# Absorbed queries of the third layer by halves of TensorE's rows: four products of 224 columns in place of two of 448

## The chip, the core and the metric

The kernel runs on one core of a Trainium2 chip. The metric is the device time of one execution in microseconds (us); the time of a kernel is the median of several runs. A profiled execution is one further run, recorded by the hardware profiler.

## What is computed

Sixteen sequences of 56 tokens and width 256 pass through four layers, each with cross-attention to a context of 1500 rows of width 128 (`ctx_1024`). The change lies in the third layer (`_L2_xattn_ref`), in its cross-attention with 16 heads of width 8:

```
ckv = encoder_outputs @ ckv_w
ck, cv = jnp.split(ckv, 2, axis=-1)
cq, ck, cv = heads(ci @ cq_w), heads(ck), heads(cv)
cctx = sdpa(cq, ck, cv, causal=False)
hidden_states = hidden_states + merged(cctx) @ cdense_w
```

The kernel does not make the keys. Since `q . (ctx W_k)` is `(q W_k^T) . ctx`, it multiplies each head's query by the head's eight rows of `W_k^T` (it "absorbs" the key weights into the query) and takes the scores against the raw context. All of it is float32.

## The kernel before

Work goes by layer and, within a layer, by groups of `G` = 4 sequences ("batches"). `program` (line 1189) walks 16 items, layer by layer. For each item it runs the attention (`att0`, `att13`, `att2`), and beside it the closing work of the item before and the opening work of the next.

In the third layer, `keys_queries` (line 1023) prepares one batch, 16 times in all:

- It loads the turned context `kt4` (line 113).
- On GpSimd it makes `qs` (lines 1034 to 1038): the batch's 56 queries, 128 rows of 16 heads x 8, repeated for four heads at a time with all rows but the head's own set to zero by the mask `m_heads`. There are four such operations, one for each group `g` of four heads, each with 56 x 4 = 224 columns. In every column only eight of the 128 rows are not zero.
- On TensorE it multiplies two groups at a time (448 columns, 128 rows) by the stationary `ckT`, which is `W_k^T` (line 1041). There are two products for a batch, each into its own buffer `t` in PSUM.
- On ScalarE it copies each result of 448 columns to `qa` (line 1045).

`att2` (line 1090) then runs the scores in periods. One block of `scores_block` (line 339) is four products of 375 columns, one for each quarter of the context, each on 32 columns of the array (the profile writes 128*32). VectorE takes mask and maximum (line 344), ScalarE the exponentials (line 381), VectorE turns the blocks (line 392), and line 1133 forms the weighted sums. `own_sums` (line 1062) closes a batch: its product at line 1071 also goes to a buffer `t`, and VectorE reads that at line 1076. `keys_queries` for the next batch is called in the middle of a batch (line 1115).

Two things set the order around the change. The pool of `t` has two buffers (line 79, `turn` at line 93), which `shift_of` (lines 361 and 373), `values` (line 1055), `own_sums` and `keys_queries` share. And the order on each engine is not the order of the source: the framework's scheduler lays it out when the program is built, by the order of the source, its own durations and the time at which buffers come free in its plan. On the chip each engine then keeps that order, and each instruction waits for its semaphores.

Two more places take part in the argument. `absorbed` (line 692) does the same for the second and fourth layers, with heads of width 64: it already uses the upper or the lower 64 rows of the array (64*128), two halves in two buffers `t`, 112 columns in each product (line 702). And the program holds two variants of itself behind a branch; with these inputs the first one runs (the score tile `ktl` of line 138 is its mark).

Of the kernel before, what the change touches and what calls it, by code (L numbers as in the profile page):

```python
# [9 lines left out]
F32 = mybir.dt.float32  # L10
# [10 lines left out]
B, N, M = 16, 56, 1500  # L21
# [9 lines left out]
NB, BW = 12, 32  # L31
# [8 lines left out]
QC = R // 4  # L40
# [22 lines left out]
def tile_kernel(ctx: ExitStack, tc: tile.TileContext, a, layers=4, groups=NG):  # L63
# [3 lines left out]
    nc = tc.nc  # L67
# [4 lines left out]
    mpool = ctx.enter_context(tc.tile_pool(name="mask", bufs=2))  # L72
# [10 lines left out]
    def psum(pool, tag):  # L83
        return pool.tile([128, 512], F32, tag=tag, name=tag)
# [8 lines left out]
    def turn():  # L93
        return psum(ps_t, "t")
# [16 lines left out]
    def load_kt4(b):  # L111

        kt = kpool.tile([DM, NQ, QB], F32, tag="kt", name="kt4")
        nc.sync.dma_start(kt, a["ctxT4"][b])
        return kt
# [57 lines left out]
    def load_x(gi):  # L173
# [5 lines left out]
    ident = const.tile([128, 128], F32, name="ident")  # L179
    make_identity(nc, ident)  # L180
    sizes = {
        "hm": 26, "m_own": 4, "m_head": BW, "m_eight": 8, "causal": N, "vecs": 22,
        "gates": 4, "rope": 33, "m_mine": H, "m_half": 128, "m_same": BW,
    }
    tables = const.tile([128, sum(sizes.values())], F32, name="tables")
# [4 lines left out]
    hm, vecs, gates = views["hm"], views["vecs"], views["gates"]  # L190
    m_own, m_head, m_eight = views["m_own"], views["m_head"], views["m_eight"]
    causal, tab = views["causal"][:TP], views["rope"][:N]
    m_mine, m_half, m_same = views["m_mine"], views["m_half"], views["m_same"]
    m_self, m_two, m_heads = hm[:, 0:8], hm[:, 8:10], hm[:, 10:26]
    l2w = const.tile([128, 512], F32, name="l2w")
    ckT, cv, cd = l2w[:, :DM], l2w[:, DM : 2 * DM], l2w[:, 2 * DM :]
    no_mask = const.tile([128, QW], BF16, name="no_mask")
# [46 lines left out]
    def scalar_copy(out, in_, scale=1.0):  # L244
        nc.scalar.activation(out, in_, AF.Copy, scale=scale)  # L245
# [777 lines left out]
    def keys_queries(b, state):  # L1023
        made = {}
        state["made"][b % G] = made
        kt = load_kt4(b)
        made["kt"] = kt
        qa = big.tile([128, 2 * R], F32, tag="qa", name="qa2")[:, : 4 * QC].rearrange(
            "p (g n) -> p g n", g=4
        )  # L1030
        made["q"] = qa
        qs = mpool.tile([128, 4, N, 4], F32, tag="mb", name="qs")
        cq = state["cq"][:, b % G * N : (b % G + 1) * N]
        for g in range(4):
            nc.gpsimd.tensor_tensor(
                qs[:, g], cq.unsqueeze(2).to_broadcast([128, N, 4]),
                m_heads[:, 4 * g : 4 * g + 4].unsqueeze(1).to_broadcast([128, N, 4]), ALU.mult,
            )
        for g in range(0, 4, 2):
            p = turn()  # L1040
            nc.tensor.matmul(
                p[:, : 2 * QC], ckT, qs[:, g : g + 2].rearrange("p g n h -> p (g n h)"),
                start=True, stop=True,
            )
            scalar_copy(qa[:, g : g + 2], p[:, : 2 * QC].rearrange("p (g n) -> p g n", g=2))

    def values(made):

# [35 lines left out]
    def first2(gi, state):  # L1084

        cross[gi] = state
        state["made"] = {}
        keys_queries(gi * G, state)

    def att2(gi, state, then, side, ends, last):  # L1090
# [13 lines left out]
        for n in range(per * G):  # L1104
# [4 lines left out]
            if k == 0:  # L1109
                values(made)  # L1110
                den = few_sums()[:, : N // 2].rearrange("p (i g) -> p i g", g=4)
                sums = mpool.tile([128, N, 4], F32, tag="own", bufs=1, name="sums")
            elif k == 2:
                if b + 1 < G:
                    keys_queries(gi * G + b + 1, state)
                else:
                    then()
# [137 lines left out]
def constants():  # L1255

    import numpy as np

    p = np.arange(128)
    head_masks = np.concatenate(  # L1260
        [
            p[:, None] // 16 == np.arange(8), p[:, None] % 32 // 16 == np.arange(2),
            p[:, None] // 8 == np.arange(16),
        ],
        axis=1,
    ).astype(np.float32)

    own = (p[:, None] // 8 % 4 == np.arange(4)).astype(np.float32)  # L1270
    d = np.arange(32)
    head = (p[:, None] % 4 == d // 8).astype(np.float32)
    eight = (p[:, None] % 32 // 4 == np.arange(8)).astype(np.float32)
    t = np.arange(N)
    causal = np.where(t[:, None] >= t[None, :], 0.0, -BIG).astype(np.float32)
    inv = np.float32(1.0) / np.float32(10000.0) ** (np.arange(0, 16, 2, dtype=np.float32) / np.float32(16))
    freqs = np.outer(t.astype(np.float32), inv).astype(np.float32)
    c, s = np.cos(freqs), np.sin(freqs)
    table = np.concatenate([c, c, -s, s, t[:, None]], axis=1).astype(np.float32)

    mine = (p[:, None] % 32 // 2 == np.arange(16)).astype(np.float32)
    half = (p[:, None] % 2 == np.arange(128) // 64).astype(np.float32)
    same = (p[:, None] % 32 == np.arange(32)).astype(np.float32)
    return (
        head_masks, own, head, eight, np.concatenate([causal, causal]), table, mine, half, same
    )


def layout(i):
# [49 lines left out]
    )  # L1341

    masks, own, head, eight, causal, rope, *more = constants()
    vecs = np.concatenate([i[n[:2] + "_xattn" + n[2:]].reshape(2, 128) for n in VEC]).T
    gates = np.concatenate([i[n[:2] + "_xattn" + n[2:] + "_gate"] for n in GATE]).reshape(1, 4)
# [29 lines left out]
```

## Time and profile before

| | us |
|---|---|
| runs: median of 3 (lowest to highest) | 1768.75 (1766.23 to 1775.0) |
| profiled execution, its own time | 1774.53 |
| its span, first to last instruction | 1772.7 |
| around the span | 1.8 |
| PE busy in the span | 1668.2 (94%) |
| DVE busy | 1126.1 (64%) |
| ACT busy | 1022.1 (58%) |
| POOL busy | 112.1 (6%) |
| third layer, about 500 to 1340 us: PE busy | 810.6 of 840.0 |

How to read it: PE is TensorE's products, PEld its loads of stationary operands (they overlap products), DVE is VectorE, ACT is ScalarE, POOL is GpSimd. A float32 product appears as two records, each with its own load. A group's row gives, after the count, the busy time, the mean of one in ns, and the idle time before it with what ended it. The duration of a PE record runs from its start to its modelled end and so contains the array's depth; what a product costs the engine is the step from one start to the next.

### The profile page before, as it was taken

Reading aid. Unit: us, or ns where it says so; the run is one execution under the profiler, and the core shown is the slowest. Engines: PE = TensorE matmul, PEld = TensorE weight load, DVE = VectorE, ACT = ScalarE, POOL = GpSimd, SP = SyncE. Lnnn points to the kernel's source line nnn. Section 1 sums busy time; section 2 is a strip of 40 time slices with the busy share of each in tenths; the row PEclk is TensorE's granted clock in tenths of the full one; section 3 lists DMA queues with packets and bytes.
Section 4 is the critical chain, followed back from the end, with each engine's and each line's share of the span. In section 5 each row is a group of like instructions: output and inputs, shape, how many; then the busy total and the mean of one; then the engine's idle time right before and its main releaser. Section 6 shows DMA issues by size and latency. Waiting matters only on the chain.

```text
span 1772.7 us, 55493 instructions
## 1 busy us (share of the span) xinstructions
PE 1668.2 (94%) x23964; PEld 1104.3 (62%) x23964; DVE 1126.1 (64%) x2742; ACT 1022.1 (58%) x3580; POOL 112.1 (6%) x238
## 2 busy tenths in 40 slices
PE   4888999999999999999999999999999999999997
PEld 2566777776664556545665556556656777777765
DVE  2344866657765666777657776576488746666672
ACT  1443976757454446553755547457555876766663
POOL 0000000000011000110000000000000000000000
PEclk9999999999999999999999999999999999999998
DMA  6431203020030121000210002211200132212120
GB/s 175 126 109 45 77 24 108 25 89 25 14 133 28 43 97 46 21 20 20 99 69 20 20 20 99 74 38 43 99 21 16 48 119 64 76 52 89 44 68 8
DMA packets 60132, 106.80 MB, mean 60 GB/s; under 512 B 7430, under 2 KB 44950, under 8 KB 59878
## 3 DMA queue, kind: packets, MB, share of 16 engines
q1 hardware_dynamic: 58726, 97.01, 17.0%
q0 software_dynamic: 1152, 6.14, 1.4%
q8 instruction: 190, 3.11, 0.7%
q14 instruction: 64, 0.52, 0.1%
HBM read 102.23 MB, written 0.92 MB: 58 GB/s over the span
## 4 chain that ended last, share of the span: by engine, by line
PE 77%; DVE 12%; ACT 6%; DMA 3%; issue 2%; POOL 1%; SPq 0%; POOLq 0%; DVEq 0%
PE sc L339 21%; PE o L795 9%; PE mm L1166 4%; ACT p L381 4%; PE o L1133 4%; DVE p L392 4%; PE mm L858 3%; PE mm L846 3%; PE mm L831 3%; PE mm L682 3%; PE mm L1179 2%; PE t L702 2%; DVE p L344 2%; PE t L1055 2%; PE t L743 2%; PE t L751 2%
## 5 line engine op out<-in xcount | busy, mean ns | idle before, releaser
L381 ACT ACTIVATE p<-p,few 128x96 f32<-128x96 f32 (+1 forms) x1344 | 588.3, 440 | 3.8
L339 PE MATMUL sc<-kt,qa 128*32 128x375 f32 x3584 | 407.8, 486 | 5.1 <-issue 3.1
L392 DVE STREAM_TRANSPOSE p<-p 128x480 f32<-128x480 f32 (+3 forms) x319 | 316.5, 1003 | 53.0 <-ACT p L381 52.1
L344 DVE CUSTOM_DVE_ANT_0 p<-sc,no_mask 128x375 f32<-128x375 f32 x448 | 236.4, 536 | 95.1 <-PE sc L339 86.3
L381 ACT ACTIVATION_READ_ACCUMULATOR p<-p,few 128x1 f32 x1344 | 252.2, 188 | 0.0
L339 PE MATMUL sc<-ktl,qa 128*32 128x96 f32 x7168 | 200.1, 249 | 2.3 <-issue 1.6
L339 PEld LDWEIGHTS sc<-kt,qa 128*32 128x32 f32 x3584 | 126.8, 109 | 107.7 <-issue 70.1
L1133 PEld LDWEIGHTS o<-p,vc 128*32 128x32 f32 x6144 | 142.9, 110 | 75.8 <-issue 51.2
L339 PEld LDWEIGHTS sc<-ktl,qa 128*32 128x32 f32 x7168 | 157.7, 110 | 34.0 <-issue 17.3
L795 PE MATMUL o<-p,kvl 128*128 128x448 f32 x384 | 167.9, 565 | 1.2 <-DVE p L392 1.2
L1133 PE MATMUL o<-p,vc 128*32 128x64 f32 (+1 forms) x6144 | 159.7, 215 | 8.7 <-DVE p L392 7.1
L245 ACT ACTIVATE few<-t 128x14 f32<-128x14 f32 (+2 forms) x128 | 22.2, 174 | 212.7 <-PE t L373 212.7
L350 DVE TENSOR_TENSOR p<-sc,mkl 128x480 f32<-128x480 f32 (+1 forms) x192 | 113.6, 607 | 25.5 <-PE sc L339 25.3
L354 DVE TENSOR_REDUCE few<-p 128x5 f32<-128x480 f32 (+1 forms) x192 | 114.4, 612 | 2.8
L795 PEld LDWEIGHTS o<-p,kvl 128*128 128x128 f32 x384 | 67.0, 191 | 55.3 <-issue 44.7
L245 ACT ACTIVATE qa<-t 128x224 f32<-128x224 f32 (+1 forms) x96 | 38.4, 420 | 91.4 <-PE t L702 62.7
L1166 PE MATMUL mm<-xT,w 128*128 128x224 f32 (+1 forms) x384 | 81.0, 360 | 1.1 <-DVE h2T L1171 0.9
L1166 PEld LDWEIGHTS mm<-xT,w 128*128 128x128 f32 (+1 forms) x384 | 65.7, 178 | 15.6 <-DVE h2T L1171 5.3
L1055 PE MATMUL t<-l2w,kt 128*32 128x128 f32 x1536 | 60.2, 275 | 6.2 <-issue 5.8
L245 ACT ACTIVATE ot<-o 128x448 f32<-128x448 f32 x64 | 33.8, 527 | 54.0 <-PE o L795 54.0
L702 PE MATMUL t<-qT,wl 64*128 64x112 f32 x512 | 55.4, 284 | 3.2 <-DVE qa L713 2.0
L757 DVE TENSOR_TENSOR oT<-t,over 128x224 f32<-128x224 f32 x64 | 31.8, 551 | 41.3 <-PE t L751 38.2
(262 smaller groups left out, 2293.8 us busy)
## 6 DMA issues: line engine op xcount, KB each, us to landing
w<-in_L_W SPq DMA_DIRECT2D x16, 1024.0 KB
kt<-in_ctxT SPq DMA_DIRECT2D x16, 768.0 KB
w<-in_L_Wq SPq DMA_DIRECT2D x8, 1024.0 KB
w<-in_L_Wo SPq DMA_DIRECT2D x8, 1024.0 KB
ktl<-in_ctxT SPq DMA_DIRECT2D x32, 192.0 KB
kvl<-in_ctx_last SPq DMA_DIRECT2D x32, 192.0 KB
w<-in_L_v_qkv SPq DMA_DIRECT2D x4, 768.0 KB
w<-in_L_l_qkv SPq DMA_DIRECT2D x4, 768.0 KB
```

What stands on the lines that cost most here:

```text
L245: nc.scalar.activation(out, in_, AF.Copy, scale=scale)
L339: nc.tensor.matmul(sc[g * BW : (g + 1) * BW, at : at + w], q, k, start=True, stop=True, skip_group_check=True,)
L344: return nc.vector.tensor_tensor_reduce(u["p"][:, i, :w], sc[:, :w], u["mask"], 1.0, LOWEST, ALU.add, ALU.max, u["mx"][:, i : i + 1],).ins ...
L350: nc.vector.tensor_tensor(p, sc[:, : m * w].rearrange("p (i k) -> p i k", i=m), u["mask"].unsqueeze(1).to_broadcast([128, m, w]), ALU.add,)
L354: return nc.vector.tensor_reduce(u["mx"][:, i : i + m], p, AX.X, ALU.max).ins.name
L381: nc.scalar.activation(u["p"][:, i, : u["w"]], u["p"][:, i, : u["w"]], AF.Exp, bias=u["shift"][:, i : i + 1], accum_out=u["den"][:, i : i ...
L392: turned = nc.vector.transpose(blocks, blocks)
L702: nc.tensor.matmul(halves[e][:, j * TP : (j + 1) * TP], wkT[e * 64 : (e + 1) * 64, j0 + j, :], qT[e * 64 : (e + 1) * 64, j0 + j, tok], sta ...
L795: nc.tensor.matmul(o[:, : ub * BW], kv[:, j, :], p, start=start, stop=stop)
L1055: nc.tensor.matmul(p[g * BW : (g + 1) * BW, (j - j0) * DM : (j - j0 + 1) * DM], made["kt"][:, g, j * BW : (j + 1) * BW], cv, start=True, s ...
L1133: nc.tensor.matmul(o[cols, : pieces * BW], made["v"][:, j, cols], p.rearrange("p (i g) r -> p g i r", g=4)[:, g], start=start, stop=stop, ...
L1166: nc.tensor.matmul(p[:w, k * T : (k + 1) * T], wt[:, c, cols], xe[n][:, c, :], start=(c == 0), stop=(c == 1),)
```

## The change

- The mask `m_heads` has 8 columns in place of 16: row `p` counts as head `p // 8 % 8`. The table in memory is narrower by 8 columns.
- `qs` has two groups in place of four. One GpSimd operation now serves two groups of heads at once, since heads `h` and `h + 8` lie in different halves of the rows: two operations for a batch in place of four, of the same 224 columns.
- In place of two products of 448 columns over 128 rows there are four of 224 columns over 64 rows each (`ckT[rows]`, `qs[rows, g]`). Both buffers `t` are taken first. In the source the products alternate: lower half and upper half for `g` = 0, then the same for `g` = 1.
- ScalarE copies as before, two results of 448 columns, now one for each half.

```
-        qs = mpool.tile([128, 4, N, 4], F32, tag="mb", name="qs")
+        qs = mpool.tile([128, 2, N, 4], F32, tag="mb", name="qs")
         cq = state["cq"][:, b % G * N : (b % G + 1) * N]
-        for g in range(4):
+        for g in range(2):
             nc.gpsimd.tensor_tensor(
                 qs[:, g], cq.unsqueeze(2).to_broadcast([128, N, 4]),
                 m_heads[:, 4 * g : 4 * g + 4].unsqueeze(1).to_broadcast([128, N, 4]), ALU.mult,
             )
-        for g in range(0, 4, 2):
-            p = turn()
-            nc.tensor.matmul(
-                p[:, : 2 * QC], ckT, qs[:, g : g + 2].rearrange("p g n h -> p (g n h)"),
-                start=True, stop=True,
-            )
-            scalar_copy(qa[:, g : g + 2], p[:, : 2 * QC].rearrange("p (g n) -> p g n", g=2))
+        halves = [turn(), turn()]
+        for g in range(2):
+            for e in range(2):
+                rows = slice(e * 64, (e + 1) * 64)
+                nc.tensor.matmul(
+                    halves[e][:, g * QC : (g + 1) * QC], ckT[rows],
+                    qs[rows, g].rearrange("p n h -> p (n h)"), start=True, stop=True,
+                )
+        for e in range(2):
+            scalar_copy(
+                qa[:, 2 * e : 2 * e + 2],
+                halves[e][:, : 2 * QC].rearrange("p (g n) -> p g n", g=2),
+            )
...
-            p[:, None] // 8 == np.arange(16),
+            p[:, None] // 8 % 8 == np.arange(8),
```

The built program's order on TensorE, in the variant that runs, is this for a typical batch (buffer, source, output form; line numbers moved by up to 7: 1041 became 1044, 1133 became 1140):

```
before:  L1041 t_7472<-qs 128x448
         L339 sc<-kt4,qa2 32x375 x5
         L1041 t_7475<-qs 128x448
after:   L1044 t_7470<-qs 128x224 x2
         L339 sc<-kt4,qa2 32x375 x5
         L1044 t_7471<-qs 128x224 x2
```

Each buffer name stands for one half. Of the 16 batches, 14 have this form (both products of one half, other work, both products of the other half), one has both products of one half and then, at once, both of the other, and one (the second batch) has the halves alternating.

More of the change, by code (lines that the diff above doesn't have):

```diff
@@ L181, in tile_kernel @@
     sizes = {
-        "hm": 26, "m_own": 4, "m_head": BW, "m_eight": 8, "causal": N, "vecs": 22,
+        "hm": 18, "m_own": 4, "m_head": BW, "m_eight": 8, "causal": N, "vecs": 22,
         "gates": 4, "rope": 33, "m_mine": H, "m_half": 128, "m_same": BW,
@@ L193, in tile_kernel @@
     m_mine, m_half, m_same = views["m_mine"], views["m_half"], views["m_same"]
-    m_self, m_two, m_heads = hm[:, 0:8], hm[:, 8:10], hm[:, 10:26]
+    m_self, m_two, m_heads = hm[:, 0:8], hm[:, 8:10], hm[:, 10:18]
     l2w = const.tile([128, 512], F32, name="l2w")
```

## The prediction

> **What bounds the kernel now.** I read the page first: busy times, slices, and the chain of work that ended last.
>
> ```profile
> span 1772.7 us, 55493 instructions
> ...
> PE   4888999999999999999999999999999999999997
> PEld 2566777776664556545665556556656777777765
> DVE  2344866657765666777657776576488746666672
> ACT  1443976757454446553755547457555876766663
> POOL 0000000000011000110000000000000000000000
> PEclk9999999999999999999999999999999999999998
> ...
> PE 77%; DVE 12%; ACT 6%; DMA 3%; issue 2%; POOL 1%; SPq 0%; POOLq 0%; DVEq 0%
> ```
>
> TensorE is busy in 90% or more of nearly every slice, at its full clock, and holds 77% of the chain. The third layer fills slices 12 to 30. There a saved microsecond of TensorE is worth up to a microsecond, while GpSimd has a tenth of its time in use and 1% of the chain. Second, the groups by line, for the operations that the change touches:
>
> ```profile
> L702 PE MATMUL t<-qT,wl 64*128 64x112 f32 x512 | 55.4, 284 | 3.2 <-DVE qa L713 2.0 <-DVE oT L757 0.9 <-ACT few L245 0.3
> L1035 POOL TENSOR_TENSOR qs<-l,tables 128x224 f32<-128x224 f32 x64 | 37.4, 615 | 78.1 <-PE t L1041 35.7 <-ACT l L245 33.4 <-DVE p L350 9.0
> L1041 PE MATMUL t<-qs,l2w 128*128 128x448 f32 x64 | 31.6, 581 | 0.7
> L1041 PEld LDWEIGHTS t<-qs,l2w 128*128 128x128 f32 x64 | 9.9, 188 | 10.7 <-ACT qa L245 6.7 <-issue 1.2 <-DVE over L1076 1.1
> ```
>
> The 32 products of line 1041 are 64 records; nothing makes TensorE idle long before them (0.7 us), so all that they take is on the path. It is 1.8% of the span: the prize is half of it. Third, the timeline of TensorE, where the start of a row less that of the row before is what the earlier one costs. First one batch of the third layer:
>
> ```profile
> 704.39 1.02 PE L1041 MATMUL t<-qs,l2w 128*128 128x448 f32 x2
> 705.34 1.45 PE L339 MATMUL sc<-kt,qa 128*32 128x375 f32 x10
> 706.88 1.02 PE L1041 MATMUL t<-qs,l2w 128*128 128x448 f32 x2
> 707.83 0.84 PE L339 MATMUL sc<-kt,qa 128*32 128x375 f32 x8
> ```
>
> A product costs 0.95 us. The single records' starts divide this: 0.480 to its second record and 0.469 to the scores, where two records between untiled neighbours step by 0.376. So 0.75 us is streaming and about 0.10 each is paid on entering from, and leaving to, the array in columns. Then two places of line 702, which already works in halves of the rows:
>
> ```profile
> 228.85 1.14 PE L702 MATMUL t<-qT,wl 64*128 64x112 f32 x8
> 229.92 0.29 PE L339 MATMUL sc<-ktl,qa 128*32 128x96 f32 x4
> ...
> 270.74 1.15 PE L702 MATMUL t<-qT,wl 64*128 64x112 f32 x16
> 271.81 0.37 PE L339 MATMUL sc<-ktl,qa 128*32 128x96 f32 x8
> ```
>
> This is the row that decides. Eight records of one half alone take 1.07 us; sixteen, eight of each half, take 1.07 us too. Halves share the time only when both are in the queue together; one half alone leaves the other idle.
>
> **The change, part by part.** *TensorE's order.* In the source the halves alternate. In the built order they do so in one batch of 16. A batch starts with `own_sums` (line 1071) holding one of the two buffers `t` until VectorE has read it, so the scheduler finds a buffer for the lower half, issues both its products, then scores, and the upper half only when ScalarE has copied the lower. In 14 batches other work stands between the halves, in one (the third) the second half waits for VectorE. So the half alone is the case that counts.
>
> *Cost of a half alone.* It is four records of 224 columns. Records of 224 columns step by 0.189 us (lines 682, 846 and 1166 in their runs). A lone half of line 702 pays 0.088 on entering and 0.090 on leaving: 8 x 0.112 + 0.178 = 1.07, as above. So 4 x 0.189 + 0.178 = 0.934 us, against 0.949.
> - 22 products stand between column-tiled work on both sides: 22 x (0.934 - 0.949) = -0.33 us.
> - Four (at 540.5, 546.0, 784.5 and 1002.0 us) follow untiled work and cost 0.845 now. The half must be entered also from there: line 702 after line 954 starts 0.523 later where the untiled step is 0.429. That is 0.094 + 0.934 - 0.845 = +0.18 each, +0.73 us.
> - Two (1141.5 and 1216.5 us) leave to untiled work at 0.856: +0.08 each, +0.16 us.
> - The second batch (579.8 us), halves alternating: two products cost 1.55 us now. Together: 0.094 to enter, two steps of 0.189, 0.178: 0.65 us. Gain 0.90 us, or 0.6 if the upper half starts 0.3 late, as some of line 702's do. I take -0.90.
> - The third batch (644.8 us) takes 1.69 us now, a wait of 0.08 included; two halves one after the other give the same, up to 0.19 less if the last record of the first overlaps. I take 0.
>
> Sum on TensorE: -0.34 us.
>
> *Weight loads.* They double, 64 more records of about 188 ns. One rule speaks against this change. The row first: lone halves of line 702 step by 0.112 us although each load lasts 0.187; eight loads alone would be 1.5 us and the eight records took 1.07. So loads lie under products of the same half. The Trainium skill ("TensorE: Matmul & The Clock Gate", section "The mechanism", on what overlaps) says that a load overlaps running products only when it targets another group of rows. By that rule and the page's load time (columns divided by 1.2 GHz: 0.107 us for 128), a record of 224 columns would step by about 0.296 and the product of 448 by 0.480; a batch half would cost 4 x 0.296 against 2 x 0.480, +0.22 us, and all 32 together +7 us. The row shows 0.376 for the product of 448, and its streaming alone is that (0.189 for half the columns), so no load is in the open. I take the row: 0 us.
>
> *GpSimd.* 32 operations of 0.59 us fall away (19 us of its time). They wait for TensorE or ScalarE, not the reverse: before line 1041 TensorE waited for ScalarE and VectorE, 8 us in all, never for `qs`. In the first batch the lower half needs both new operations, as the first product needed two of the four. Worth 0; without the cover (the half batch of work that lies between) a batch would gain at most two operations, 1.1 us. The shorter table load is 4 KB of 107 MB: 0.
>
> *ScalarE and buffers.* The two copies of 448 columns (543 ns) stay and stand at the same places; the lower half's copy holds back the upper half as the first copy held back the second product (9 waits, 6.7 us in all). Nothing new queues behind them. 0.
>
> *Moved steps.* Elsewhere the order is the same but for single instructions, except from 645 to 690 us. There all four turns of line 252 now stand together and wait for VectorE, the weighted sums and line 846 are interleaved differently, the 0.77 us of scores between line 846 and line 858 comes after line 858 (which waits for Gelu), and ScalarE loads one more table (1.28 us). TensorE is busy in 68.0 of the 70 us from 640 to 710, so a gain is at most 2.0 us, and a loss is bounded by the cover taken away (0.8) plus the table (1.3). I take +0.8, nearest to the row of 0.77.
>
> Total: -0.34 + 0.8 = +0.5 us. On the profiled execution, 1774.5 us by its own time (span 1772.7 and 1.8 around it), that is 1775.0. The median of the runs, 1768.75, is lower by 5.8 us, so I apply the difference to it: **1769.2 us**, no change that could be seen. About 0.5% (8.8 us) is what a measurement of this kernel can tell.
>
> **Rivals.**
> *The halves run together as the source has them* (faster). For: line 702 does it at 270.74 us with no loss. Then a pair costs 2 x 0.189 + 0.178 = 0.56 against 0.95, 0.39 us x 32 = 12.5 us: **1756.3 us**. Against: it needs both buffers free at once; the built order has it in one batch. It would take the engine passing scores that stand ahead in the queue.
> *The loads come into the open* (slower). Place: each half's second, third and fourth record, on the same 64 rows. Price: 64 additional loads x 188 ns = 12.0 us: **1780.8 us**. It decides from 8.8 / 64 = 0.14 us for each additional load, that is, when records in a half step by 0.33 instead of 0.19. By the page's smaller price it is 1775.7 and still within the bound. Against: the 0.112 of line 702.
> *GpSimd's lighter load counts* (slightly faster): 1.1 us in each of the batches where TensorE waits for `qs`; that could be the first alone, so 1768 us, not told from no change.
>
> **How the numbers follow.** The likeliest, halves one after the other at today's price: 0.82, about 1764 to 1777 (the moved steps' bounds -2.0 and +2.1, and the runs of before, which alone spread over 1766.2 to 1775.0). Halves together: 0.07. Loads in the open beyond the bound, or a worse stall in the moved steps: 0.11. The range is widened a little toward both other cases, 1761 to 1778. Faster 0.07, same 0.82, slower 0.11.
>
> **What would show it.** In the changed profile, line 1044 should have 128 records of 224 columns with form 64*128, steps of 0.189 in a half, and busy about the old 31.6 us (30 to 33); rows of it with four records, each starting 0.93 us before the next line's row, and in one place (near 580 us) eight records in 0.65 us. Busy near 18 us would mean halves together; steps of 0.3 or more, loads in the open. GpSimd's row should halve to about 19 us with no change of TensorE's waits. The prediction is wrong if TensorE's busy time or idle time in 640 to 710 us moves by more than 2 us, or if a wait for line 1036 appears before line 1044.

## The result and the profile after

| | before | after |
|---|---|---|
| median of 20 runs each, us | 1769.55 | 1776.19 |
| lowest to highest, us | 1763.48 to 1775.0 | 1767.85 to 1794.85 |
| ratio, 95% interval | | 1.0041 (1.0027 to 1.0055) |
| profiled execution, us (span) | 1774.53 (1772.7) | 1772.88 (1771.1) |
| mean granted clock (before: 47 runs beside the first four experiments; after: without its slowest run) | 0.9879 | 0.9866 |

The change costs 0.4%, about 7 us. One of the changed kernel's 20 executions (1794.85 us, clock 0.978) was in a slower state and is left out of the ratio. The cost is within the 0.5% that the forecast allowed for "no change that could be seen", but the interval leaves out 1, and the sum of the prediction had +0.5 us. The two profiled executions stand the other way round, 1.6 us in favour of the changed kernel. They are one execution each, so the 7 us cannot be read off by laying one against the other.

First the page of the changed kernel: span, TensorE's slices and granted clock, and the engines' shares of the chain.

```profile
span 1771.1 us, 55589 instructions
...
PE   3888999999899999999999999999999899999997
...
PEclk9999999999999999999999999999999999999999
...
PE 76%; DVE 12%; ACT 6%; DMA 2%; issue 2%; POOL 1%; SPq 0%; POOLq 0%; DVEq 0%; ACTq 0%
```

Nothing new bounds the kernel: TensorE is as full as it was, and no other engine has gained a share of the chain. There are 96 more instructions, which is what 64 more records of products, 64 more loads and 32 fewer operations of GpSimd make. Next the groups by line of the changed kernel, for what the diff replaced.

```profile
L1044 PE MATMUL t<-qs,l2w 64*128 64x224 f32 x128 | 31.5, 375 | 0.9 <-ACT qa L245 0.3
L1044 PEld LDWEIGHTS t<-qs,l2w 64*128 64x128 f32 x128 | 20.7, 186 | 11.5 <-ACT qa L245 7.2 <-issue 1.3 <-DVE over L1083 0.8
L1036 POOL TENSOR_TENSOR qs<-l,tables 128x224 f32<-128x224 f32 x32 | 20.1, 648 | 81.3 <-PE t L1044 37.7 <-ACT l L245 33.5 <-DVE p L350 10.0
```

There are 128 records of 64 rows and 224 columns, busy for 31.5 us where 64 records were busy for 31.6. The loads have doubled in number and in time, and the idle time before the products is 0.9 us where it was 0.7. GpSimd has half its operations, and line 1036 is not among what TensorE waited for. Third, the timeline of TensorE in the changed kernel: the second batch, the third batch and a typical one.

```profile
577.06 1.88 PE L954 MATMUL mm<-w,xT 128*112 128x512 f32 x4
578.87 1.03 PE L1044 MATMUL t<-qs,l2w 64*128 64x224 f32 x8
579.83 0.82 PE L339 MATMUL sc<-kt,qa 128*32 128x375 f32 x2
...
642.27 1.86 PE L1044 MATMUL t<-qs,l2w 64*128 64x224 f32 x8
644.06 0.60 PE L252 MATMUL mm<-ident,xn 112*128 112x112 f32 x4
...
738.26 1.02 PE L1044 MATMUL t<-qs,l2w 64*128 64x224 f32 x4
739.21 1.45 PE L339 MATMUL sc<-kt,qa 128*32 128x375 f32 x10
740.75 1.02 PE L1044 MATMUL t<-qs,l2w 64*128 64x224 f32 x4
```

In the typical batch (738.26) a half takes 739.21 - 738.26 = 0.95 us, as long as a product of 448 columns over all rows took; the other half follows 2.5 us after the first. In the second batch, where the halves alternate, eight records take 0.96 us: both halves at the price of one. In the third batch they stand one after the other, 1.79 us.

### The profile page after: what moved, and what is told of

Same layout as the page of the kernel before. It is cut to its first block, busy times and chain, and to the rows that moved or that the text cites. A ratio compares the mean times of both kernels' runs of the same rounds, so it can differ in the third digit from the quotient of the medians.

```text
span 1771.1 us, 55589 instructions
## 1 busy us (share of the span) xinstructions
PE 1666.0 (94%) x24028; PEld 1111.1 (63%) x24028; DVE 1124.8 (64%) x2742; ACT 1023.9 (58%) x3581; POOL 95.1 (5%) x206
## 4 chain that ended last, share of the span: by engine, by line
PE 76%; DVE 12%; ACT 6%; DMA 2%; issue 2%; POOL 1%; SPq 0%; POOLq 0%; DVEq 0%; ACTq 0%
PE sc L339 21%; PE o L795 8%; ACT p L381 4%; PE mm L1173 4%; PE o L1140 4%; DVE p L392 4%; PE mm L858 3%; PE mm L846 3%; PE mm L831 3%; PE mm L682 3%; PE mm L1186 2%; PE t L702 2%; DVE p L344 2%; PE t L1062 2%; PE t L743 2%
## 5 line engine op out<-in xcount | busy, mean ns | idle before, releaser
L350 DVE TENSOR_TENSOR p<-sc,mkl 128x480 f32<-128x480 f32 (+1 forms) x192 | 113.7, 607 | 26.1 <-PE sc L339 25.8
L1062 PEld LDWEIGHTS t<-l2w,kt 128*32 128x32 f32 x1536 | 45.8, 111 | 21.8 <-issue 17.8
```

The costliest lines, as they stand in the source:

```text
L350: nc.vector.tensor_tensor(p, sc[:, : m * w].rearrange("p (i k) -> p i k", i=m), u["mask"].unsqueeze(1).to_broadcast([128, m, w]), ALU.add,)
L1062: nc.tensor.matmul(p[g * BW : (g + 1) * BW, (j - j0) * DM : (j - j0 + 1) * DM], made["kt"][:, g, j * BW : (j + 1) * BW], cv, start=True, s ...
```

## Experiments: where 7 us come from

The prediction's own sum left more than 6 us unexplained. The first theory was that the moved steps between 645 and 690 us cost it all. Its rivals were the products themselves, the mere number of instructions on TensorE, and GpSimd's new operations.

The ratios below are to before, from runs on the same chip; they need not be the quotient of the medians. All were on one chip but `e12`, which with its runs of before was on another. Before itself had 1768.44 us beside the first four kernels, 1767.50 beside the next four, 1768.00 beside `e9`, `e10` and `e11`, and 1767.72 beside `e12`.

**One product of 448 columns for each half** (`e1_half448`). TensorE has before's instructions in before's order; only the rows of these products differ.

```
-        halves = [turn(), turn()]
-        for g in range(2):
...
         for e in range(2):
+            rows = slice(e * 64, (e + 1) * 64)
+            p = turn()
+            nc.tensor.matmul(
+                p[:, : 2 * QC], ckT[rows], qs[rows].rearrange("p g n h -> p (g n h)"),
+                start=True, stop=True,
+            )
```

> The halves of the rows and the two GpSimd operations are kept, but each half is one product of 448 columns, so no product is added and TensorE's order is that of the kernel before, instruction for instruction. Three theories of the +0.4%. Moved steps (the order from 645 to 690 us): gone here, ratio to the kernel before 1.000. More instructions (64 more records with their loads, more code to fetch and more stalls without a visible wait): gone too, 1.000. The half array itself costs more than its steps show: stays, 1.004. By the steps of the changed kernel a half of 448 columns should cost 2 x 0.376 + 0.18 = 0.93 to 0.95 us, as the product before.

Measured: 1769.89 us, ratio 1.0006 (0.9989 to 1.0024). The group by line of this kernel:

```profile
L1043 PE MATMUL t<-qs,l2w 64*128 64x448 f32 x64 | 31.3, 588 | 0.8
```

It shows that half the rows save nothing while the other half has nothing to do: 64 records, 31.3 us, against 31.6 us for all rows. The slowdown is gone as well. So neither the halves as such nor GpSimd's two operations (this kernel has them too) make the 7 us.

**Each product of before cut into two of 224 columns, over all rows** (`e2_split224`). There are no halves here, and TensorE's order is that of the changed kernel, moved steps included.

```
         for g in range(0, 4, 2):
             p = turn()
-            nc.tensor.matmul(
-                p[:, : 2 * QC], ckT, qs[:, g : g + 2].rearrange("p g n h -> p (g n h)"),
+            for k in range(2):
+                nc.tensor.matmul(
+                    p[:, k * QC : (k + 1) * QC], ckT,
+                    qs[:, g + k].rearrange("p n h -> p (n h)"), start=True, stop=True,
...
```

> The kernel before, with each product of 448 columns over all 128 rows made as two of 224; four GpSimd operations stay. It has the changed kernel's number of products and its order on TensorE, moved steps included, but no halves. Moved steps and more instructions: both give the changed kernel's ratio, 1.004. The half array: gone, 1.000 to 1.001.

Measured: 1775.01 us, ratio 1.0038 (1.0022 to 1.0054), the changed kernel's slowdown without any half. What costs is the longer stream of instructions or its order.

**The changed kernel with before's order from 645 to 690 us** (`e3_but_third`). One batch uses a single product of 448 columns for each half, and this is enough for the scheduler to lay out that stretch as before.

```
+        w = 2 if b == 2 else 1
-        for g in range(2):
+        for g in range(0, 2, w):
...
-                    halves[e][:, g * QC : (g + 1) * QC], ckT[rows],
+                    halves[e][:, g * QC : (g + w) * QC], ckT[rows],
...
```

> The changed kernel, but in the third batch of each group each half is one product of 448 columns; this gives back the order of the kernel before from 645 to 690 us, while most of the additional products stay (48 of 64 records). Moved steps: ratio 1.000 to 1.001, and 644.8 to 704.4 us takes 59.6 us as before instead of 61.0. More instructions: 1.003. The half array: 1.004.

The edit reaches only the third batch of the first group, so 60 of the 64 additional records stay, not 48 as the text above says. Measured: 1777.96 us, ratio 1.0061 (1.0037 to 1.0085), above what any of the three theories gave, though the interval reaches down to 1.004. The stretch did come back. These are the starts of the third batch's products and of the next batch's, in before, in the changed kernel and here:

```profile
644.83 1.85 PE L1041 MATMUL t<-qs,l2w 128*128 128x448 f32 x4
704.39 1.02 PE L1041 MATMUL t<-qs,l2w 128*128 128x448 f32 x2
```

```profile
642.27 1.86 PE L1044 MATMUL t<-qs,l2w 64*128 64x224 f32 x8
703.23 1.02 PE L1044 MATMUL t<-qs,l2w 64*128 64x224 f32 x4
```

```profile
640.07 1.85 PE L1045 MATMUL t<-qs,l2w 64*128 64x448 f32 x4
699.80 1.02 PE L1045 MATMUL t<-qs,l2w 64*128 64x224 f32 x4
```

From the one to the other, at full clock in all three, it is 59.56 us in before, 60.96 in the changed kernel and 59.73 here. So the moved steps are worth 1.4 us, and the slowdown stays without them. The first theory falls.

**Four GpSimd operations in the changed kernel** (`e4_pool4`), with TensorE's order untouched.

```
-        qs = mpool.tile([128, 2, N, 4], F32, tag="mb", name="qs")
+        qs = mpool.tile([128, 4, N, 4], F32, tag="mb", name="qs")
...
-        for g in range(2):
+        for g in range(4):
...
-                m_heads[:, 4 * g : 4 * g + 4].unsqueeze(1).to_broadcast([128, N, 4]), ALU.mult,
+                m_heads[:, 4 * (g % 2) : 4 * (g % 2) + 4].unsqueeze(1).to_broadcast([128, N, 4]), ALU.mult,
...
```

> The changed kernel with four GpSimd operations for a batch instead of two (the two additional ones write columns of qs that nothing reads); TensorE's order is that of the changed kernel. All theories: the changed kernel's ratio, 1.004, since GpSimd's lighter load was worth nothing. If GpSimd mattered, it would be slower still, by up to 1 us for each batch (1.01).

Measured: 1778.47 us, ratio 1.0055 (1.0037 to 1.0074). GpSimd has its old load back and the slowdown is still there: GpSimd is not it.

**A new theory: where the packets of code fall.** TensorE stands still at a few places, with "issue" as the reason, that is, with nothing it waits for. This is such a place in before, and then one in the changed kernel, each on TensorE's timeline; the bracket is the idle time before the row.

```profile
937.11 1.27 PE L1055 MATMUL t<-l2w,kt 128*32 128x128 f32 x38
940.95 0.41 PE L1055 MATMUL t<-l2w,kt 128*32 128x128 f32 x3 [2.57 <-issue]
```

```profile
934.48 0.50 PE L1062 MATMUL t<-l2w,kt 128*32 128x128 f32 x7
938.22 2.14 PE L1062 MATMUL t<-l2w,kt 128*32 128x128 f32 x34 [3.24 <-issue]
```

The work stops in the middle of a run of equal products, after 38 of them in one kernel and after 7 in the other. Equal products just before and after it ran without a wait, and the profile shows none here; the theory is that instructions are missing. The stretches of the changed kernel around it (length, busy time by engine, granted clock, the DMA engines' busy share, GB/s) show what else goes on:

```profile
933.00:936.00 3.00, 1.78 (x83) 1.33 (x72) 2.48 (x9) 2.08 (x8) 0.16 (x1) 1.00 0.72 259
936.00:938.00 2.00, 0.00 (x0) 0.00 (x0) 1.39 (x1) 2.00 (x7) 0.00 (x0) 0.96 0.00 0
938.00:941.00 3.00, 2.78 (x44) 2.58 (x47) 0.38 (x1) 1.92 (x7) 0.00 (x0) 0.50 0.02 5
```

From 933 to 936 the DMA engines bring in the next turned context, 768 KB in about 3 us. Code comes by DMA too. The page of the changed kernel has its instructions by engine and this queue (packets, MB, share of the 16 engines):

```profile
PE 1666.0 (94%) x24028; PEld 1111.1 (63%) x24028; DVE 1124.8 (64%) x2742; ACT 1023.9 (58%) x3581; POOL 95.1 (5%) x206
...
q8 instruction: 191, 3.13, 0.7%
```

That is 191 packets of 16 KB, and they are TensorE's: a straight line through them, in before and in the changed kernel, gives one packet for every 256 of its instructions (products, loads and waits). About half of them start 5 to 10 us after the one before. The packet due here is recorded at 935.98, as the load ends, 11.6 us after the one before it, and takes 0.96 us. TensorE goes on at 938.2; the next packet follows after only 3.4 us. All standstills on "issue" of over 0.7 us in the third layer of the two profiles go this way (us from the start of the span):

| kernel | load | code packet starts | TensorE stands |
|---|---|---|---|
| before | 719.5 to 722.5 | 722.3 | 721.9 to 724.6 |
| before | 757.0 to 760.0 | 760.1 | 761.0 to 762.6 |
| before | 935.5 to 938.5 | 938.5 | 938.4 to 940.9 |
| before | 1154.0 to 1157.0 | 1157.2 | 1158.1 to 1159.5 |
| after | 753.5 to 756.5 | 756.5 | 756.4 to 758.8 |
| after | 933.0 to 936.0 | 936.0 | 935.0 to 938.2 |
| after | 973.0 to 976.0 | 976.0 | 976.5 to 978.4 |
| after | 1189.0 to 1192.0 | 1191.7 | 1192.2 to 1193.9 |

Not every packet in such a place stops TensorE. In before 14 packets of the third layer start during one of these loads or within 1 us behind it, in the changed kernel 12, and only four of each go with a standstill. What sets these apart is how late they are. Count TensorE's instructions up to the start of a packet, take off 256 for each packet before it, and call the median of the third layer zero: the eight packets of the table come 241 to 254 instructions late, a whole packet's worth, the other 18 at most 203. So it looks as if TensorE stands where it has used up the code that it had.

A standstill can have an echo: the last row of the stretches has the clock at 0.50. The theory: each 16 KB of code ends at a fixed count of instructions, so any added instruction moves the edges of all later packets against the loads; and a packet that falls due at the wrong place in a load comes so late that TensorE stops. The 64 records and 64 loads that the change adds are half a packet. The rival: more instructions cost time by themselves, wherever the edges fall. Two kernels tell them apart by adding still more instructions.

**32 products of one number each at the start** (`e5_before_s32` on before, `e6_after_s32` on the changed kernel). They are 64 records and 64 loads, half a packet of code, and run while the first loads come in; the rest of the order stays.

```
+        room = mm()
+        for _ in range(32):
+            nc.tensor.matmul(room[:1, :1], ident[:, :1], ident[:, :1], start=True, stop=True)
         load_first()
```

> The kernel before with 32 products of one number each put ahead of everything on TensorE, while it waits for its first data; the order of all else on TensorE is unchanged. Program code reaches TensorE in packets of 16 KB, and these products move the place of every later packet's edge in the program by half a packet or so. Phase of the code packets (stalls come where a packet falls behind a context load; which ones do so depends on the edges): the stalls of the third layer move to other batches, and the time moves by up to 0.4% in either direction (1762 to 1776). Number of instructions in the third layer, or the half array: 1.000, stalls where they were.

> The changed kernel with the same 32 products ahead. Phase of the code packets: the stalls leave the places of the changed kernel, the time moves by up to 0.4% in either direction, most likely down, since the changed kernel has drawn an unlucky phase (1.000 to 1.004 of the kernel before). Number of instructions: stays at 1.004 to 1.006.

Measured: before with them 1773.19 us, ratio 1.0019 (1.0003 to 1.0035); the changed kernel with them 1767.40 us, ratio 0.9994 (0.9978 to 1.0009). The same harmless addition slows the one by 0.2% and takes the whole 0.4% from the other. A cost by number of instructions cannot do that; a shift of packet edges can. In the profile of the changed kernel with the addition, all standstills named in the table are gone, and two of 0.97 and 0.73 us are left. In before with it they moved too, to these two places:

```profile
972.44 0.75 PE L1055 MATMUL t<-l2w,kt 128*32 128x128 f32 x20 [1.43 <-issue]
...
1189.87 0.59 PE L1055 MATMUL t<-l2w,kt 128*32 128x128 f32 x9 [2.20 <-issue]
```

They add up to 3.6 us, where before's four have 8.3, and yet the runs are slower. So standstills are not the whole account. The mean clock of these runs is 0.9854, that of before beside them 0.9884; what that is worth stands further down.

**Both halves side by side** (`e7_stand448`, `e8_ownmm448`). These test the prediction's rival: one product of 448 columns for each half, tied in the scheduler so that the second follows the first at once. In the first kernel the pair waits until `own_sums` has given its buffer back; in the second `own_sums` takes its buffer from the pool `mm` instead.

```
+        before_it = line["over"]
...
-                    halves[e][:, g * QC : (g + 1) * QC], ckT[rows],
-                    qs[rows, g].rearrange("p n h -> p (n h)"), start=True, stop=True,
+                    halves[e][:, : 2 * QC], ckT[rows],
+                    qs[rows].rearrange("p g n h -> p (g n h)"), start=True, stop=True,
...
+                    tc.add_manual_dep(product.ins, before_it,
...
+                before_it = product.ins.name
```

```
+        before_it = None
...
-        t = turn()
+        t = mm()
```

> Halves as one product of 448 columns each, and tied in the schedule so that they are laid out only once VectorE has read the buffer of own_sums: in 12 batches the two halves stand next to each other. If halves share the array's time as those of line 702 do, an adjacent pair takes about 0.95 us in place of 1.90, so 12 x 0.95 = 11 us less, minus 0 to 4 us for the wait for the second buffer and for scores that are moved: ratio 0.994 to 0.998. If halves do not share time: 1.000 to 1.003.

> Halves as one product of 448 columns each; own_sums takes its buffer from the pool of mm, so that both buffers t are free when the halves are due; in nearly all batches they stand next to each other. If halves share time: 14 to 16 x 0.95 = 13 to 15 us less, against what the busier pool of mm costs the side work (0 to 10 us): ratio 0.992 to 1.000. If halves do not share: 1.000 to 1.006.

Measured: the first 1761.61 us, ratio 0.9959 (0.9945 to 0.9972); the second 1785.29 us, ratio 1.0085 (1.0066 to 1.0104). On TensorE's timeline of the first, a pair that finds both buffers free, and one that doesn't:

```profile
742.44 2.14 PE L1045 MATMUL t<-qs,l2w 64*128 64x448 f32 x4
744.51 0.54 PE L1150 MATMUL o<-p,vc 128*32 128x64 f32 x24
...
849.38 1.02 PE L1045 MATMUL t<-qs,l2w 64*128 64x448 f32 x4
850.33 0.48 PE L1150 MATMUL o<-p,vc 128*32 128x64 f32 x19
```

At 849.38 two halves take 0.95 us together; their single records start at 0, 6, 480 and 486 ns, in step. At 742.44 the same four take 2.07 us, since the second had to wait for its buffer. The gain that the halves hold depends on order alone. The kernel has little of it yet: in five of the 16 batches the second half starts within 0.11 us of the first, in six it is next in line but starts 0.5 to 1.2 us after it, and in five other work stands between. Up to the next row the products take 26.1 us, where before's took 29.2, so 3.1 of the 5.9 us between the medians are the halves'. The tie moved other work as well, and where the rest comes from no run separates.

The second kernel is slower than both its expectations allowed. Here the halves share their time in ten batches and their products take 21.6 us, but TensorE is without work for 123 us of its span (1783.5 less 1660.2 busy), against 108 in the first of the two and 105 in before. That the side work which the pool `mm` serves runs later is the likely reason; no row here shows it.

**The standstills taken away.** In `e9_noload` fifteen of the sixteen loads of the turned context are left out; in `e10_pieces` each goes as four transfers of 192 KB. The first leaves all batches with the first one's context. TensorE's order is the changed kernel's in both.

```
+    once = const.tile([DM, NQ, QB], F32, name="once")
...
-        kt = load_kt4(b)
+        if "kt4" not in line:
+            line["kt4"] = once
+            nc.sync.dma_start(once, a["ctxT4"][b])
+        kt = once
```

```
-        nc.sync.dma_start(kt, a["ctxT4"][b])
+        for g in range(NQ):
+            nc.sync.dma_start(kt[:, g], a["ctxT4"][b][:, g])
```

> The changed kernel, but the third layer reads one batch's turned context for all 16 batches: 15 of its 16 loads of 768 KB are left out (so the keys and values of those batches are another batch's). TensorE's order is unchanged. Code packets that fall behind these loads: no stall of TensorE over 0.7 us without a visible wait is left between 600 and 1340 us, and the time falls by the 7 to 9 us that such stalls took, and by half-clock windows that followed them: ratio to the kernel before 0.994 to 0.998. Stalls from code alone, with no part in them of the loads: the stalls stay, 1.003 to 1.006.

> The changed kernel with each load of 768 KB issued as four of 192 KB (one for each quarter of the context, packets of 1.5 KB in place of 6 KB); TensorE's order is unchanged. If a code packet can slip in between the pieces, stalls shrink to under 1 us each: 0.998 to 1.001 of the kernel before. If it waits for all that is queued, stalls stay or grow with the longer load: 1.004 to 1.008.

Measured: without the loads 1767.10 us, ratio 0.9992 (0.9978 to 1.0007); in pieces 1765.91 us, ratio 0.9986 (0.9972 to 1.0000). Both take away the 0.4%. The first was expected to gain more, 0.994 to 0.998. TensorE's timeline at the place of the 3.24 us, in the kernel without loads and then in the one with pieces:

```profile
934.19 1.27 PE L1066 MATMUL t<-l2w,once 128*32 128x128 f32 x39
935.20 0.48 PE L340 MATMUL sc<-once,qa 128*32 128x375 f32 x1
```

```profile
935.06 1.27 PE L1063 MATMUL t<-l2w,kt 128*32 128x128 f32 x39
936.07 0.48 PE L340 MATMUL sc<-kt,qa 128*32 128x375 f32 x1
```

The run that was cut after 7 products goes through 39 without a gap. The first kernel has no standstill of over 0.7 us left in the third layer, the second has one (1.22 us, at 1150.3).

**Pieces alone, on before, and on the pairs** (`e12_before_pieces`, `e11_stand448_pieces`), with the edit just shown.

> The kernel before with its context loads of the third layer in four pieces; TensorE's order is unchanged. It takes the code stalls out of the kernel before too, so that against the changed kernel with the same loads (0.9986 of the kernel before, 1765.9 us) only the change itself is left. By the rows that is +1.4 us for the moved steps and +0.6 us for products and entries: this kernel should take about 1764 us, 0.9975 of the kernel before. If the change costs nothing by itself: 0.9986.

> Halves next to each other as in the tied version, and the load in four pieces. If pieces let code through: 0.992 to 0.995 of the kernel before; if not: 0.996 to 1.000.

Measured: before with pieces 1765.81 us, ratio 0.9995 (0.9983 to 1.0007), which misses its expectation. Two standstills of 1.3 us are left in its profile (715.8 and 1285.0), where before had four of 1.5 to 2.7. The runs gain little by it, at a mean clock of 0.9875 where before's beside them had 0.9892; why the clock was lower is not known. The pairs with pieces take 1759.21 us, ratio 0.9955 (0.9937 to 0.9974), the fastest kernel here, by 0.45% over before and a little short of what was expected; what the pieces add to the pairs is within the intervals. The two kernels with pieces are the fair comparison of the change: 0.9986 against 0.9995 leaves it at -0.09%, give or take 0.18%, so the +2.0 us that the measured terms below give (0.11%) lie just outside, and no loss of 0.4% is left.

## Why the prediction was right or wrong

- **Halves one after the other, no gain: right.** Line 1044's steps in a half alone are 293, 189, 190 and 279 ns, 0.951 us in all. The term was 0.934; entering costs 0.104 where line 702 gave 0.088. Over 22 halves that is 22 x (0.951 - 0.949) = +0.04 in place of -0.33 us.
- **The second batch: a mis-sized term.** It was put at 0.65 us, "two steps of 0.189". A half has four records, not two, since each float32 product is two: with four steps the same sum is 0.094 + 4 x 0.189 + 0.178 = 1.03, and 0.094 + 0.957 = 1.05 was measured. The gain there was 1.55 - 1.05 = 0.50 us, not 0.90, and below the 0.6 that the prediction named as the lower end. The rival "halves together" errs less: its 0.56 us is the price of four records, charged 32 times with entering and leaving each time. Eight records in a row pay that once: both halves take 0.95 us for a batch, against 1.90 for two products, so the rival was worth 0.95 x 16 = 15 us and not 12.5; the pairs of `e7_stand448` that find their buffers free show the price.
- **Entries and exits from untiled work** cost 0.094 us each, as put. All products together: the rows of line 1044 take 29.37 us up to the next row, those of line 1041 took 29.22, and five entries come on top (the second batch's included), 5 x 0.094. That is +0.6 us where the sum had -0.34; 0.1 of it is the third batch, 1.79 against 1.69 us, which was put at 0.
- **Weight loads: right.** The steps of 0.189 us stand beside loads of 0.186 us for the same 64 rows. The rule of the Trainium skill ("TensorE: Matmul & The Clock Gate", section "The mechanism"), that a load overlaps only products on other rows, would have made them about 0.296 by the prediction's estimate. The same section also lets a load into the background weight buffer go ahead, and the steps fit that sentence. The row decided rightly, and the slower rival falls with it.
- **GpSimd, ScalarE and buffers: right.** GpSimd's row fell from 37.4 to 20.1 us without effect, and with four operations instead of two the ratio was 1.0055, within the intervals the same as 1.0041.
- **Moved steps: +1.4 us, not +0.8**, within their bounds (-2.0 to +2.1).
- **What failed is the step from the sum to the total.** It took the rest of the kernel to run as it ran in the profile of before, and put the whole difference into the operations named in the diff. So the standstills for code and the clock, which no term holds, were put at nothing. By measured terms the change is 0.6 + 1.4 = +2.0 us (the third batch's 0.1 stands in both). The medians differ by 6.6. The remaining 4.6 us vanish, and within the intervals the 2.0 with them, when other instructions move the packet edges (`e6_after_s32`), when the loads are left out, and when they are cut. So much is shown: the loss depends on where the code's edges fall and on loads of 768 KB, and the 32 additional products, with their loads half a packet of code, moved those edges. That the range held the time was luck: its width came from the bounds of the moved steps and the spread of before's runs, and nothing in it stood for this cause.

A part of these 4.6 us came by way of the clock. A line through the other 19 runs of the changed kernel (without the one of 1794.85 us) gives about 2 us for each 0.001 of mean clock; 0.9866 against 0.9879 is thus worth 2.6 us, and the clock of `e5_before_s32`, 0.9854 against 0.9884, all that it lost. The mean is 0.9885 without loads and 0.9889 in pieces. The clock is not wholly a cause of its own here, since a standstill can lower it.

The profiles of the eleven kernels without pairs show both parts side by side, each in one execution:

| kernel | span, us | standstills over 0.7 us in the third layer, sum in us | us at half clock in the span |
|---|---|---|---|
| before | 1772.7 | 8.3 | 50.1 |
| after | 1771.1 | 9.2 | 37.9 |
| `e1_half448` | 1765.2 | 6.6 | 39.9 |
| `e2_split224` | 1764.8 | 8.7 | 31.0 |
| `e3_but_third` | 1771.5 | 6.9 | 46.8 |
| `e4_pool4` | 1775.1 | 11.6 | 41.3 |
| `e5_before_s32` | 1772.9 | 3.6 | 60.5 |
| `e6_after_s32` | 1766.7 | 1.7 | 43.1 |
| `e9_noload` | 1765.3 | 0 | 41.6 |
| `e10_pieces` | 1767.4 | 1.2 | 43.5 |
| `e12_before_pieces` | 1758.9 | 2.6 | 33.2 |

As an estimate from these rows (least squares), a microsecond of standstill lengthens the span by 0.8 us (standard error 0.2) and one at half clock by 0.43 (0.09); what is left scatters by 2.3 us. That also answers why the two first profiles stand the wrong way round: the one of before has 0.9 us less of standstills and 12 us more at half clock.

What stays open: there is one profile of each kernel, and the standstills add up to nearly the same for before and after. Before's profile is one of its slower executions, 1774.53 us against a median of 1769.55, so its 8.3 us need not be usual; the difference of the medians rests on the kernels that move or remove the standstills, and how often which one occurs in a usual run was not seen. Not all time at half clock follows a standstill, and what else moves it from kernel to kernel is not known. And why a packet of code that falls into a load mostly starts only at its end (behind it in each DMA engine, or asked for too late) no run here separates.

## What to carry to other kernels

Half of the array's rows is worth something only if the other half works at the same time; look for that in the built order, not in the source, and where two buffers decide it, tie the pair (here -0.4% where the untied change gave +0.4%, though only about half of the gain was traced to the halves). Before a difference of a few tenths of a per cent is put down to an edit that adds instructions, move the code by some harmless instructions and measure again. Standstills on "issue" in the middle of equal products, beside a large load, can be missing code: look for its packet there, and try the load in pieces.

## What was not expected of the hardware

- A code packet of 16 KB (256 instructions of TensorE) that starts only as a load of 768 KB ends can stop TensorE: for 1.4 to 3.2 us in the eight cases of before and after, in which it came 241 to 254 instructions late. TensorE goes on 1.2 to 1.6 us after such a packet has landed (it takes 0.9 to 1.0 us). With loads of 192 KB one gap of 1.2 us was left in the changed kernel and two of 1.3 us in before.
- After a standstill the clock can be at half for a while: 0.50 from 938 to 941 us in the changed kernel after 3.24 us, and 0.50 from 941 to 944 us in before after 2.57 us. The Trainium skill ("TensorE: Matmul & The Clock Gate", section "What's actually happening") speaks of an idle window of about 3.4 us; here less standing still was enough.
- Two halves of 448 columns started 6 ns apart and took 0.952 us; one alone took 0.946.
